# Graph-layer kernel: the left-over sums read all 128 rows of the last chunk, GpSimd zeroes its empty rows, and block A's second layer moves to right behind them

## The chip, the cores and the metric

The kernel runs on one core of one Trainium2 chip. The metric is the device time of the whole kernel in microseconds, over several runs; three runs of the kernel before lie between 277.67 and 277.8 us.

## The reference

There are 12500 nodes with 128 features, 412500 edges with 48 features, and for each edge the number of its receiving node. The edges are sorted by receiver.

```python
h   = jnp.maximum(_layernorm(x), 0.0)
agg = jax.ops.segment_sum(edges, recv, num_segments=12500)    # 48 per node
u   = graph_globals[0]                                         # the same for every node
hid = jax.nn.relu(concat([h, agg, u]) @ W1 + b1)               # 256 per node
out = x + hid @ W2 + b2
```

All numbers are 32-bit floats.

## The kernel before, in words

**Chunks, groups, blocks.** 768 edges are a chunk: it lies in SBUF as 128 rows of 6 edges. Four chunks are a group, loaded by one transfer of 576 KB. Eleven groups and 1024 nodes make an iteration; there are 12 of them (`NIT`), and in each two blocks of 512 nodes, A and B, go through the layers. Behind the 12 iterations come the left-overs: six chunks, five of them whole (`FULL` is 5) and the last with 84 edges, which fill only 14 of its 128 rows (`TP` is 14), and a last block Z of 212 nodes.

**What one iteration does.** VectorE (DVE) writes a one-hot tile per slot of groups (L662: 28 columns, 1 where an edge's receiver has that distance from the chunk's start). TensorE (PE) multiplies it with the edges, six products per chunk, four chunks side by side in four column ranges (L681), so that a PSUM bank S holds sums of the edges by receiver; ScalarE (ACT) copies them out (L685). DVE writes a second kind of one-hot tile, `pl` (L668), which shifts the 28 sums of each chunk to the right place among the iteration's nodes, and PE adds them up in two banks (L703). Beside that the nodes are normalised (DVE, ACT), turned by PE (L740), and go through the first layer (L750 for the nodes, L755 for the sums, `relu` on ACT, L760). The second layer (`second`, L772) is 16 matmul records per block (L776) and an addition on DVE: in the loop it writes the block of the iteration before into `hold` (L780), in the epilogue into `ot` (L778). What it adds is `xb`, the block's input plus the bias b2, which GpSimd (POOL) makes in `add_b` (L735); GpSimd may do so only when the addition of the iteration before has read the old `xb`.

**Stores are kept back.** 11 of the 12 iterations' results stay in SBUF in `hold`, and are stored in the epilogue: `store_held` (L783) issues 22 stores of 256 KB on the SP queue, one behind the other. The last blocks are stored by `store` (L560): A and Z on the SP queue behind those, B on ACT's. So all of the 6.4 MB of output leave in the epilogue.

**What sets the order.** Each operation is recorded by `op(engine, name, reads, writes, ...)`. An engine runs its operations in the order in which they are recorded. A wait is derived from the names: an operation waits for the last writer of what it reads or writes, and for the readers of what it writes. Each engine except PE runs the iterations as a loop and then the epilogue's operations; PE's loop is rotated but comes to the same order. A transfer waits on its issuing engine's queue, and everything behind it on that queue waits with it.

**The epilogue** (L926). `load_rest` (L544) records on SP the transfer `lez`, five whole chunks, 720 KB, into `e[0]`, and then `lezt`, the last chunk's 14 rows, 15.8 KB. `e[0]` is the edge tile of slot 0; `lez` waits until the last iteration's sums over slot 0 (`su0`) have read it. `lezt` names `e0.1` as `lez` does, and so waits until `lez` has landed. Then come the 22 stores. `sur` (L937 to L940) is the left-over sums on PE. Its 36 products, 72 matmul records in the trace, are 24 of the first four chunks and then 6 + 6 of the fifth and the sixth chunk in turn, the latter over 14 rows alone (`rest`, L936). ACT copies them (`ssr`, L941). PE goes on with the last shifted sums of the loop (`place(5, (0,), 0)`), the turning of Z, the shifted left-over sums (`pcr`, L948), Z's first layer, block A's second layer, a transposition for the verdict on whether the sorted edges were dense enough (L632), block B's second layer, and Z's. `verdict_0` and `verdict_1` are small DVE operations.

Of the kernel before, what the change touches and what calls it, by code (L numbers as in the profile page):

```python
# [18 lines left out]
P = 128  # L19
EPS = 1e-5  # L20
T = 6
CE = P * T
CG = 4
# [3 lines left out]
IN = 1024  # L27
# [7 lines left out]
V = 28  # L35
NV = 32
# [16 lines left out]
class Flow:  # L53
# [14 lines left out]
    def op(self, eng, name, reads, writes, emit, dma=False):  # L68
        self.seq.append(dict(eng=eng, name=name, r=tuple(reads), w=tuple(writes), emit=emit, dma=dma, it=self.at))
# [336 lines left out]
def kernel(  # L406
# [12 lines left out]
    nc = tc.nc  # L419
    N, D = x.shape  # L420
    E, DE = edge_attr.shape
# [7 lines left out]
    TP = TAIL // T  # L429
# [14 lines left out]
    def bank(name):  # L444
        return psum.tile([P, BN], F32, name=name)

    S = [bank("s0"), bank("s1")]
    agg = [bank("ax"), bank("ay")]
    pt = bank("pt")
    ph = [bank("ph0"), bank("ph1")]  # L450
# [9 lines left out]
    e = [const.tile([P, len(p) * CG, T * DE], F32, name=f"e{s}") for s, p in enumerate(SLOTS)]  # L460
    oh = [const.tile([P, len(p) * q, V], F32, name=f"oh{s}") for s, p in enumerate(SLOTS)]
# [48 lines left out]
    op = f.op  # L510
    A, B, Z = 0, 1, 2

    def dma(eng, name, reads, writes, dst_ap, src_ap):
        def emit(i):
            with nc.allow_non_contiguous_dma(reason="small pieces"):
                return [f.of[eng].dma_start(dst_ap(i) if callable(dst_ap) else dst_ap, src_ap(i) if callable(src_ap) else src_ap)]  # L516
        op(eng, name, reads, writes, emit, dma=True)
# [24 lines left out]
    FULL = NFULL - (NIT * GI + 1) * CG  # L542

    def load_rest():  # L544
        at = (NIT * GI + 1) * GE
        dma("SP", "lez", [], ["e0.0", "e0.1"], e[0][:, :FULL], edge_attr[at:at + FULL * CE].rearrange("(c p t) d -> p c (t d)", p=P, t=T))
        dma("SP", "lezt", [], ["e0.1", "ezt"], e[0][:TP, FULL], edge_attr[E - TAIL:E].rearrange("(p t) d -> p (t d)", t=T))

    def rows_of(ap, i, a, m, r):
        return span(ap, i, a, m * r).rearrange("(p r) d -> p (r d)", r=r)  # L550
# [9 lines left out]
    def store(k, a, m=P, eng="SP"):  # L560
        r = RR[k]
        dv = ot[k].rearrange("p r d -> p (r d)")
        q = m - m % 16
        dma(eng, f"so{k}", [f"ot{k}"], [], lambda i: rows_of(out, i, a, q, r), dv[:q])
        if q < m:
            dma(eng, f"so{k}t", [f"ot{k}"], [], lambda i: rows_of(out, i, lambda i: a(i) + q * r, m - q, r), dv[q:m])
# [42 lines left out]
    def farthest():  # L609

        op("DVE", "fa", ["rel_i"], ["far"], lambda i: [nc.vector.tensor_reduce(
            far, rel_i.rearrange("p g t -> p (g t)"), AX.X, OP.max, apply_absolute_value=True)])
        op("DVE", "fm", ["far"], ["farm"], lambda i: [nc.vector.tensor_tensor(farm, farm, far, OP.max)])

    def verdict_0():
        v0 = NG - 1
        live = NV * (NCH - v0 * CG)
        vs = [f"vv{b}" for b in range(NB)]
        op("DVE", "w0", vs, ["worst1"], lambda i: [nc.vector.tensor_reduce(worst[:, 0:1], vv[:, :v0], AX.X, OP.max, apply_absolute_value=True)])
        op("DVE", "w1", vs, ["worst2"], lambda i: [nc.vector.tensor_reduce(worst[:live, 1:2], vv[:live, v0:NG], AX.X, OP.max, apply_absolute_value=True)])  # L620
        f.chain("DVE", "w2", ["worst1", "worst2"], ["worst"],
            lambda: nc.vector.tensor_reduce(worst[:, 2:3], worst[:, 0:2], AX.X, OP.max),
            lambda: nc.vector.tensor_scalar(worst[:, 2:3], worst[:, 2:3], -(WIN - V) / 2, None, OP.add))

    def verdict_1():
        farthest()
        f.chain("DVE", "wc", ["worst", "farm"], ["wcol"],
            lambda: nc.vector.tensor_scalar(wcol, farm, -(V - 1) / 2, None, OP.add),
            lambda: nc.vector.tensor_tensor(wcol, wcol, worst[:, 2:3], OP.max))
# [7 lines left out]
    def cols(ap, i, a, n):  # L637
        return ap[:, ds(a(i), n)] if not isinstance(i, int) else ap[:, a(i):a(i) + n]
# [52 lines left out]
    def place(s, fresh=(), part=None):  # L691

        groups, sv, pv = SLOTS[s], ss[s], pl[s]
        todo = [(n, j) + v for j, g in enumerate(groups) for n, v in enumerate(pieces(g)) if part is None or v[0] == part]
        todo.sort(key=lambda v: v[2] if len(groups) == 1 else (v[0] if v[1] == 0 else 1 - v[0], v[1]))
        seen = set()

        def emit(i):
            seen.clear()
            out = []  # L700
            for _, j, bk, at, frm, w in todo:
                h = HI * bk
                out.append(nc.tensor.matmul(agg[bk][h:h + DE, at:at + w], sv[:, j], pv[:, j, frm:frm + w],  # L703
                                            start=bk in fresh and bk not in seen, stop=True, skip_group_check=True))
                seen.add(bk)
            return out
        op("PE", f"pc{s}" + ("" if part is None else f".{part}"), [f"ss{s}", f"pl{s}"], [f"bk{b}" for b in sorted({v[2] for v in todo})], emit)
# [64 lines left out]
    def second(k, m=P, bk=None, key="PO", keep=None):  # L772

        ov = (po if bk is None else bk)[:, :RR[k] * D].rearrange("p (r d) -> p r d", r=RR[k])
        op("PE", f"w2{k}", [f"hid{k}.{a}" for a in range(NH)] + ["w2"], [key], lambda i: [
            nc.tensor.matmul(ov[:m, r], hid[k][:, a, r, :m], w2[:, a], start=(a == 0), stop=(a == NH - 1)) for r in range(RR[k]) for a in range(NH)])  # L776
        if keep is None:
            op("DVE", f"ot{k}", [key, f"xb{k}"], [f"ot{k}"], lambda i: [nc.vector.tensor_tensor(ot[k][:m], ov[:m], xb[k][:m], OP.add)])  # L778
        else:
            op("DVE", f"ho{k}", [key, f"xb{k}"] + (["spare"] if k == A else []), [f"hold{k}.{keep(f.at)}"], lambda i: [nc.vector.tensor_tensor(  # L780
                cols(hold[k], i, lambda i: keep(i) * (R * D), R * D).rearrange("p (r d) -> p r d", r=R), ov, xb[k], OP.add)])
# [144 lines left out]
    def epilogue():  # L926
        f.at = NIT
        m = RN // RZ
        load_rest()
        store_held()  # L930
        add_b(Z, m)
        stats(Z, m)
        variance(Z, m)
        shift(Z, m)
        norm(Z, m)
        rest = lambda j, c: P if j * CG + c < FULL else TP  # L936
        op("PE", "sur", ["oh0", "oh1", "e0.0", "e0.1", "ezt"], ["S0"], lambda i: [  # L937
            nc.tensor.matmul(S[0][NV * c:NV * c + V, j * DE:(j + 1) * DE], oh[j][:rest(j, c), c * T + t], e[0][:rest(j, c), j * CG + c, t * DE:(t + 1) * DE],  # L938
                             start=(t == 0), stop=(t == T - 1), skip_group_check=True)
            for j in range(2) for t in range(T) for c in range(min(CG, RC - j * CG))])  # L940
        op("ACT", "ssr", ["S0"], ["ssr"], lambda i: [nc.scalar.copy(ssr.rearrange("p j d -> p (j d)"), S[0][:, :2 * DE])])  # L941
        place(5, (0,), 0)
        turn(Z, m, S[1], "S1")
        verdict_0()
        verdict_1()
        todo = [(j,) + v for j, g in enumerate((1, 2)) for v in pieces(g)]
        op("PE", "pcr", ["ssr", "pl0", "pl1"], ["bk0"], lambda i: [
            nc.tensor.matmul(agg[bk][:DE, at:at + w], ssr[:, j], pl[j][:, 0, frm:frm + w], start=False, stop=True, skip_group_check=True)  # L948
            for j, bk, at, frm, w in todo])
        sums_out(Z, m)  # L950
        zr = [S[0][:, a * RN:(a + 1) * RN].rearrange("p (r c) -> p r c", r=RZ) for a in range(NH)]
        for a in range(NH):
            layer_x(f"z{a}", "S0", zr[a], Z, a, a == 0, m)
        for a in range(NH):
            layer_e(f"z{a}", "S0", zr[a], Z, a, m)
        for a in range(NH):
            relu(f"z{a}", "S0", zr[a], Z, a, m)
        second(A, P, ph[A], "PH0")
        store(A, lambda i: (i - 1) * IN)
        verdict_2()  # L960
        second(B, P, ph[B], "PH1")
        store(B, lambda i: (i - 1) * IN + BN, eng="ACT")
        second(Z, m, pt, "PT")
        store(Z, lambda i: i * IN, m)
        for e_ in f.of:
            op(e_, f"rb{e_}", ["bad"], [], lambda i, e_=e_: [f.of[e_].reg_load(flag_of[f.of[e_].engine], bad[0:1, 0:1])])
# [48 lines left out]
```

## Time and profile before

| | |
|---|---|
| median of three runs | 277.77 us |
| device time of the profiled execution | 277.39 us |
| its span | 275.6 us |
| granted TensorE clock | 0.973 |
| PE busy | 252.7 us, 92% |
| DVE busy | 239.5 us, 87% |
| ACT busy | 128.2 us, 47% |
| GpSimd busy | 54.5 us, 20% |
| DMA over the span | 94.33 MB, 342 GB/s |

Times in the trace are microseconds from the start of the span. The device time of the same execution is 1.8 us longer than the span. The loop ends at about 258 us for PE, and the epilogue takes the rest. A row of a timeline gives start, duration, engine, line, operation, destination and sources, shape, and how many instructions it stands for. SPq and ACTq rows are the issuing of transfers, not their flight. A row of stretches gives length, busy time of PE, its weight loads, DVE, ACT and GpSimd (instructions in brackets), the granted clock, the mean busy share of the 16 DMA engines, and what they moved in GB/s.

### The profile page before, as it was taken

To read this page: it belongs to the slowest core of one execution; us is meant where nothing else is said; L and a number is where in the kernel's file an instruction comes from. 1 tells how busy PE (TensorE), PEld (TensorE's weight loads), DVE (VectorE), ACT (ScalarE), POOL (GpSimd) and SP (SyncE) were. 2 spreads that over 40 slices of the span, in tenths; PEclk is the share of its full clock that TensorE was granted. 3 is DMA by queue.
4 is the path that set the end of the run, shared out by engine and by line. 5 is a ranking of instruction groups with operands and counts; after the bars stand their busy time and mean duration, and the time that the engine had idled before them with its cause. 6 is when DMAs were issued, how large, how long until landed. Compare 5 with 4: busy or idle time off the path is not lost.

```text
span 275.6 us, 17205 instructions
## 1 busy us (share of the span) xinstructions
PE 252.7 (92%) x7567; PEld 195.6 (71%) x7568; DVE 239.5 (87%) x591; ACT 128.2 (47%) x316; POOL 54.5 (20%) x47
## 2 busy tenths in 40 slices
PE   2946999999999999999999999999999999999990
PEld 2946866867858849859768768578498497597580
DVE  4899997998989989989989979989899899799521
ACT  7800544535437337245445355373373463454520
POOL 8100050040220400500500502304105005007000
PEclk9955999999999999999999999999999999999999
DMA  6999999999999999999999999999999999995992
GB/s 213 297 363 356 341 357 362 356 357 361 356 361 357 356 362 356 356 362 356 356 362 356 356 362 356 359 359 356 362 357 356 362 356 356 362 356 208 368 363 73
DMA packets 79012, 94.33 MB, mean 342 GB/s; under 512 B 3227, under 2 KB 72189, under 8 KB 78998
## 3 DMA queue, kind: packets, MB, share of 16 engines
q1 hardware_dynamic: 75398, 87.63, 96.1%
q10 hardware_dynamic: 3312, 6.03, 6.2%
q0 software_dynamic: 288, 0.49, 0.7%
q8 instruction: 7, 0.11, 0.2%
q14 instruction: 7, 0.06, 0.1%
HBM read 87.75 MB, written 6.40 MB: 342 GB/s over the span
## 4 chain that ended last, share of the span: by engine, by line
PE 87%; SPq 5%; DMA 3%; issue 2%; DVE 0%
PE s L681 27%; PE ph L776 18%; PE ph L750 8%; PE ax L703 7%; SPq L516 5%; PE ph L755 5%; PE po L750 4%; PE pt L750 4%; PE pt L755 4%; DMA e<-in_edge_attr_dram 3%; PE ay L703 3%; PE pt L740 3%; PE po L740 2%; PE s L938 1%; PE s L750 0%
## 5 line engine op out<-in xcount | busy, mean ns | idle before, releaser
L662 DVE TENSOR_TENSOR oh<-iota_v,rel_i 128x1344 f32<-128x1344 f32 (+1 forms) x78 | 130.8, 1716 | 0.0
L681 PEld LDWEIGHTS s<-e,oh 128*28 128x28 f32 x6336 | 75.1, 109 | 23.3 <-issue 21.4
L681 PE MATMUL s<-e,oh 128*28 128x48 f32 x6336 | 80.9, 210 | 11.0 <-issue 6.7
L735 POOL TENSOR_TENSOR xba<-xa,b_sb 128x512 f32<-128x512 f32 x12 | 15.4, 1285 | 198.3 <-DVE holda L780 198.3
L685 ACT COPY ss<-s 128x96 f32<-128x96 f32 (+1 forms) x72 | 16.8, 234 | 70.6 <-PE s L681 70.6
L668 DVE TENSOR_SCALAR pl<-iota_w,off_i 128x186 f32<-128x186 f32 x141 | 35.1, 309 | 0.5
L735 POOL TENSOR_TENSOR xbb<-xb,b_sb 128x512 f32<-128x512 f32 x12 | 31.1, 2591 | 0.0
L760 ACT ACTIVATE hida<-ph,bias 128x512 f32<-128x512 f32 x12 | 8.2, 687 | 42.2 <-PE ph L755 42.2
L703 PE MATMUL ax<-pl,ss 128*48 128x186 f32 (+3 forms) x172 | 27.1, 300 | 0.0
L776 PEld LDWEIGHTS ph<-w,hida 128*128 128x128 f32 x208 | 24.2, 191 | 3.8 <-issue 3.8
L776 PE MATMUL ph<-w,hida 128*128 128x128 f32 x208 | 26.7, 281 | 0.0
L703 PE MATMUL ay<-pl,ss 128*48 128x186 f32 (+3 forms) x168 | 26.3, 297 | 0.0
L776 PE MATMUL ph<-w,hidb 128*128 128x128 f32 x208 | 25.6, 276 | 0.6 <-issue 0.6
L776 PEld LDWEIGHTS ph<-w,hidb 128*128 128x128 f32 x208 | 24.3, 192 | 0.8 <-issue 0.7
L731 ACT ACTIVATE xna<-xa,sha,sca 128x128 f32<-128x128 f32 x48 | 19.8, 482 | 5.1 <-DVE sha L727 5.1
L710 DVE BATCH_NORM_STATS2 sta<-xa 128x6 f32<-128x128 f32 x48 | 10.5, 281 | 12.1 <-DMA xa<-in_x_dram 12.1
L703 PEld LDWEIGHTS ax<-pl,ss 128*48 128x48 f32 x172 | 17.6, 126 | 4.3 <-issue 2.0
L731 ACT ACTIVATE xnb<-xb,shb,scb 128x128 f32<-128x128 f32 x48 | 19.6, 479 | 0.0
L703 PEld LDWEIGHTS ay<-pl,ss 128*48 128x48 f32 x168 | 17.8, 124 | 0.0
L755 PE MATMUL ph<-ags,w1a 48*128 48x512 f32 x48 | 13.5, 641 | 0.0
L750 PE MATMUL ph<-hta,w1h 128*128 128x512 f32 x24 | 13.5, 644 | 0.0
L750 PE MATMUL ph<-htb,w1h 128*128 128x512 f32 x24 | 12.3, 592 | 0.0
(150 smaller groups left out, 301.5 us busy)
## 6 DMA issues: line engine op xcount, KB each, us to landing
e<-in_edge_attr_dram SPq DMA_DIRECT2D x133, 576.0 KB, 10.0
xa<-in_x_dram ACTq DMA_DIRECT2D x11, 256.0 KB, 5.8
xb<-in_x_dram ACTq DMA_DIRECT2D x11, 256.0 KB, 6.3
out_dram<-holda SPq DMA_DIRECT2D x11, 256.0 KB, 3.2
out_dram<-holdb SPq DMA_DIRECT2D x11, 256.0 KB, 3.3
holda<-in_dst_dram SPq DMA_DIRECT2D x4, 384.0 KB, 4.9
e<-in_edge_attr_dram SPq DMA_DIRECT2D x1, 720.0 KB, 8.9
xa<-in_x_dram SPq DMA_DIRECT2D x1, 256.0 KB, 10.5
```

The lines of the kernel that those rows point to most:

```text
L516: return [f.of[eng].dma_start(dst_ap(i) if callable(dst_ap) else dst_ap, src_ap(i) if callable(src_ap) else src_ap)]
L662: op("DVE", f"oh{name}", reads + ["iota_v"], [f"oh{name}"], lambda i: [nc.vector.tensor_tensor(ov, iota_v[:, None, None, :].to_broadcast([ ...
L668: nc.vector.tensor_scalar(out[:, j], iota_w, o[j], None, OP.is_equal) for j in range(len(o))])
L681: nc.tensor.matmul(S[k][NV * c:NV * c + V, j * DE:(j + 1) * DE], o[:, (j * CG + c) * T + t], ev[:, j * CG + c, t * DE:(t + 1) * DE], start ...
L685: op("ACT", f"ss{name}", [f"S{k}"], [f"ss{name}"], lambda i: [nc.scalar.copy(sv.rearrange("p j d -> p (j d)"), S[k][:, :m * DE])])
L703: out.append(nc.tensor.matmul(agg[bk][h:h + DE, at:at + w], sv[:, j], pv[:, j, frm:frm + w], start=bk in fresh and bk not in seen, stop=Tr ...
L731: nc.scalar.activation(xn[k][:m, r], xt[k][:m, r], AF.Relu, bias=sh[k][:m, r:r + 1], scale=sc[k][:m, r:r + 1]) for r in range(RR[k])])
L735: nc.gpsimd.tensor_tensor(xb[k][:m], xt[k][:m], b2_sb[:m, None, :].to_broadcast([m, RR[k], D]), OP.add)])
L740: op("PE", f"tu{k}", [f"xn{k}", "ident"], [key], lambda i: [nc.tensor.transpose(pv[:, r, :m], xn[k][:m, r], ident[:m, :m]) for r in range( ...
L750: nc.tensor.matmul(o, w1h[:, a * P:(a + 1) * P], hT[k][:, :, :m], start=first, stop=False, skip_group_check=True)])
L755: nc.tensor.matmul(o, w1a[h:h + DE, a * P:(a + 1) * P], ag[k // 2][h:h + DE, :, :m], start=False, stop=True, skip_group_check=True)])
L776: nc.tensor.matmul(ov[:m, r], hid[k][:, a, r, :m], w2[:, a], start=(a == 0), stop=(a == NH - 1)) for r in range(RR[k]) for a in range(NH)])
```

## The change

A GpSimd operation `ezz` is recorded first in the epilogue. It fills the sixth chunk's place in `e[0]`, 128 rows of 288 numbers, with zeros. It writes the name `e0.1`, so that `lez`, which writes the same name, comes behind it. `sur` then multiplies all 128 rows of each chunk. The two first verdict operations, block A's second layer and its store stand right behind `sur` and its copy, ahead of the last shifted sums and the turning of Z.

```diff
     def epilogue():
         f.at = NIT
         m = RN // RZ
+        op("POOL", "ezz", [], ["e0.1"], lambda i: [nc.gpsimd.memset(e[0][:, FULL], 0.0)])
         load_rest()
         store_held()
...
-        rest = lambda j, c: P if j * CG + c < FULL else TP
         op("PE", "sur", ["oh0", "oh1", "e0.0", "e0.1", "ezt"], ["S0"], lambda i: [
-            nc.tensor.matmul(S[0][NV * c:NV * c + V, j * DE:(j + 1) * DE], oh[j][:rest(j, c), c * T + t], e[0][:rest(j, c), j * CG + c, t * DE:(t + 1) * DE],
+            nc.tensor.matmul(S[0][NV * c:NV * c + V, j * DE:(j + 1) * DE], oh[j][:, c * T + t], e[0][:, j * CG + c, t * DE:(t + 1) * DE],
                              start=(t == 0), stop=(t == T - 1), skip_group_check=True)
             for j in range(2) for t in range(T) for c in range(min(CG, RC - j * CG))])
         op("ACT", "ssr", ["S0"], ["ssr"], lambda i: [nc.scalar.copy(ssr.rearrange("p j d -> p (j d)"), S[0][:, :2 * DE])])
+        verdict_0()
+        verdict_1()
+        second(A, P, ph[A], "PH0")
+        store(A, lambda i: (i - 1) * IN)
         place(5, (0,), 0)
         turn(Z, m, S[1], "S1")
-        verdict_0()
-        verdict_1()
...
-        second(A, P, ph[A], "PH0")
-        store(A, lambda i: (i - 1) * IN)
         verdict_2()
```

GpSimd's program from the last part of its loop into the epilogue, before. `xba` and `xbb` are the two additions of the loop, which wait for `ho0` and `ho1`, DVE's additions of the second layer; `xbr` is that of block Z.

```order
L735 TENSOR_TENSOR xba<-xa,b_sb 128x512 [waits ho0]
L735 TENSOR_TENSOR xbb<-xb,b_sb 128x512 [waits ho1]
L224 REGISTER_ALU
L746 UNCONDITIONAL_BRANCH
L230 REGISTER_ALU
L230 COMPARE_AND_BRANCH
L735 TENSOR_TENSOR xbr<-xr,b_sb 106x256 [waits lx2,lx2t]
```

The same place in the changed kernel:

```order
L735 TENSOR_TENSOR xba<-xa,b_sb 128x512 [waits ho0]
L735 TENSOR_TENSOR xbb<-xb,b_sb 128x512 [waits ho1]
L224 REGISTER_ALU
L746 UNCONDITIONAL_BRANCH
L230 REGISTER_ALU
L230 COMPARE_AND_BRANCH
L929 MEMSET e_80 128x288
L735 TENSOR_TENSOR xbr<-xr,b_sb 106x256 [waits lx2,lx2t]
```

The zeroing, L929, stands behind both additions of the last iteration.

SP's program at the start of the epilogue, before. `e_80` is `e[0]`; the first transfer is `lez`, the second `lezt`, and the stores of `hold` follow.

```order
L230 COMPARE_AND_BRANCH
L516 DMA e_80<-in_edge_attr_dram 128x5x288 [waits su0]
L516 DMA e_80<-in_edge_attr_dram 14x288 [waits lez]
L516 DMA out_dram<-holda 128x512
L516 DMA out_dram<-holdb 128x512
```

The same place in the changed kernel:

```order
L230 COMPARE_AND_BRANCH
L516 DMA e_80<-in_edge_attr_dram 128x5x288 [waits POOL]
L516 DMA e_80<-in_edge_attr_dram 14x288 [waits lez]
L516 DMA out_dram<-holda 128x512
L516 DMA out_dram<-holdb 128x512
```

`lez` waits for GpSimd's zeroing where it waited for PE's sums over slot 0; the order of the queue is the same.

PE's program in the epilogue, as a difference: `hida` is block A's hidden layer, `ph_70` the bank of its second layer.

```order
 L938 MATMUL s_65<-e_80,oh_86 28x48 x23
 L938 MATMUL s_65<-e_80,oh_87 28x48 x12
+L776 MATMUL ph_70<-w_142,hida 128x128 [waits hi0_1]
+L776 MATMUL ph_70<-w_142,hida 128x128 x7
 L703 MATMUL ax<-pl_97,ss_103 48x140
...
 L755 MATMUL s_65<-agr,w1a 128x212 [waits ACT]
 L755 MATMUL s_65<-agr,w1a 128x212
-L776 MATMUL ph_70<-w_142,hida 128x128 x8
 L632 MATMUL s_66<-ident,wcol 1x128 [waits DVE]
 L776 MATMUL ph_71<-w_142,hidb 128x128 x8
```

Block A's second layer has moved from behind Z's first layer to right behind the left-over sums. DVE's and ACT's programs have the same order as before.

## The prediction

> **What bounds the kernel now.** I read the page first, then the last 25 us. Here are the page's row of GB/s in 40 slices, its totals, and the head of the chain of work that ended last.
>
> ```profile
> GB/s 213 297 363 356 341 357 362 356 357 361 356 361 357 356 362 356 356 362 356 356 362 356 356 362 356 359 359 356 362 357 356 362 356 356 362 356 208 368 363 73
> HBM read 87.75 MB, written 6.40 MB: 342 GB/s over the span
> PE 87%; SPq 5%; DMA 3%; issue 2%; DVE 0%
> ```
>
> The chain is PE's nearly all the way, but that is a share of the whole span. The GB/s row shows two stages: loads until slice 36, a dip, and then 368 and 363 again. Behind the dip it is the output that moves: all 6.40 MB of it leave in the last 24 us. So the last stage has two candidates for its end, PE and the transfers. The rows of stretches of that stage, busy time per engine, then DMA share and GB/s:
>
> ```profile
> 246.00:247.00 1.00, 1.00 (x11) 1.00 (x11) 0.93 (x5) 0.16 (x1) 0.00 (x0) 1.00 1.09 355
> 251.20:252.00 0.80, 0.80 (x11) 0.58 (x10) 0.80 (x2) 0.75 (x2) 0.80 (x1) 1.00 0.00 0
> 252.00:252.40 0.40, 0.40 (x10) 0.34 (x7) 0.40 (x1) 0.32 (x1) 0.40 (x2) 1.00 0.18 40
> 252.40:267.80 15.40, 15.40 (x144) 10.03 (x139) 7.48 (x26) 6.19 (x14) 1.27 (x1) 1.00 0.99 374
> 267.80:268.20 0.40, 0.40 (x6) 0.40 (x6) 0.00 (x0) 0.00 (x0) 0.00 (x0) 1.00 0.26 97
> 268.20:269.00 0.80, 0.80 (x10) 0.80 (x9) 0.40 (x1) 0.00 (x0) 0.00 (x0) 1.00 0.88 333
> 269.00:270.00 1.00, 0.44 (x5) 0.23 (x3) 0.72 (x2) 0.00 (x0) 0.00 (x0) 1.00 0.01 4
> 270.20:271.40 1.20, 0.00 (x0) 0.00 (x0) 0.00 (x0) 0.00 (x0) 0.00 (x0) 1.00 0.91 306
> ```
>
> From 252.4 to 267.8 the DMA engines are full (share 0.99, 374 GB/s: 5.76 MB, which are the 22 kept stores). Only then do they idle: 0.3 us up to 268.2, 1.0 us up to 270.0. That is the whole reserve of the transfers. Now the issuing rows of the same stage, from the timeline:
>
> ```profile
> 242.25 0.72 SPq L516 DMA_DIRECT2D e<-in_edge_attr_dram  x1
> 251.22 0.36 SPq L516 DMA_DIRECT2D e<-in_edge_attr_dram  x1
> 251.62 0.37 SPq L516 DMA_DIRECT2D out_dram<-holda  x1
> 265.67 0.64 SPq L516 DMA_DIRECT2D out_dram<-holdb  x1
> 267.43 0.33 SPq L516 DMA_DIRECT2D out_dram<-ota  x1
> 269.48 0.43 DVE L778 TENSOR_TENSOR otr<-pt,xbr 106x256 f32<-106x256 f32 x1 [0.18 <-PE pt L776]
> 269.93 0.77 SPq L516 DMA_DIRECT2D out_dram<-otr  x2
> L976 SPq EVENT_SEMAPHORE  x1: 28/28/28, 272.0 to 272.0; - x1
> ```
>
> The load `lez` is issued at 242.25, in the loop's shadow; `lezt` waits for its landing until 251.22; the first kept store follows at 251.62, the last at 265.67; then SP waits for PE and DVE: A's result goes at 267.43, Z's at 269.93, and SP sees everything landed at 272.0. From there to the end of the span, 275.6, nothing is left but closing semaphores. So PE sets the end before, but the stores are only some 1.6 us behind it. SP's waits say the same:
>
> ```profile
> SPq L516 <- DMA e<-in_edge_attr_dram: 8.2, 1, 8.2
> SPq L516 <- DVE otr L778: 2.2, 1, 2.2
> ```
>
> SP's 8.2 us for `lez` cost nothing as long as the load is issued at 242; the DMA engines are still busy with edges (share 1.09 at 246).
>
> **The change part by part.** The zeroing comes first on GpSimd's epilogue. GpSimd and DVE in the last iteration:
>
> ```profile
> 248.53 1.28 POOL L735 TENSOR_TENSOR xba<-xa,b_sb 128x512 f32<-128x512 f32 x1 [15.69 <-DVE holda L780]
> 249.77 2.59 POOL L735 TENSOR_TENSOR xbb<-xb,b_sb 128x512 f32<-128x512 f32 x1
> 252.33 1.34 POOL L735 TENSOR_TENSOR xbr<-xr,b_sb 106x256 f32<-106x256 f32 x1
> 248.96 6.12 DVE L662 TENSOR_TENSOR oh<-iota_v,rel_i 128x1344 f32<-128x1344 f32 x3
> ```
>
> GpSimd stands idle for 15.69 us before `xba`, which waits for DVE's `holda`, but its program is in order: the zeroing comes behind `xbb`, at 249.77 + 2.59 = 252.36, where `xbr` starts today. `lez` waits for it, 10 us later than now. What a zeroing takes on GpSimd, from the groups by line:
>
> ```profile
> L802 POOL MEMSET ident<- 128x128 f32 x1 | 0.2, 204 | 0.5 <-SPq L980 0.5
> L820 POOL MEMSET rel<- 128x228 f32 x1 | 0.3, 307 | 0.0
> ```
>
> 100 columns more cost 103 ns, so 288 columns take about 0.37 us: it ends at 252.73. SP issues 0.02 us behind what it waits for (`otr` ends at 269.48 + 0.43 = 269.91, the store goes at 269.93), so `lez` goes at about 252.76. `xbr` shifts by 0.37 us; it is needed only for `otr` at 269.48, so that is hidden.
>
> How long `lez` flies on idle DMA engines no row shows directly. The nearest landings, and the first transfer of the program with the first DVE instruction that waited for it:
>
> ```profile
> e<-in_edge_attr_dram SPq DMA_DIRECT2D x1, 720.0 KB, 8.9
> out_dram<-ota SPq DMA_DIRECT2D x1, 256.0 KB, 2.2
> out_dram<-otr SPq DMA_DIRECT2D x1, 96.0 KB, 1.9
> 1.01 3.61 SPq L516 DMA_DIRECT2D holda<-in_dst_dram  x7
> 4.15 0.15 DVE L579 CAST fc<-holda 128x1 f32<-128x1 int32 x1 [1.21 <-DMA holda<-in_dst_dram]
> ```
>
> The 8.9 us of `lez` itself include a queue of edges in front of it, which has drained by 251.2 (share 0.00), so they are out as its price here. From below: 2.2 us for 256 KB, plus 464 KB more at 374 GB/s, 1.3 us, is 3.5. From above: the first 384 KB came in 4.15 - 1.01 = 3.1 us; 344 KB more at 355 GB/s, the rate of edge loads, are 1.0 us, so 4.1. By parts: the first store's bytes move at 252.4, 0.8 us after its issue; 737280 bytes at 355 GB/s take 2.1; and 0.6 us pass between the last bytes (271.4) and SP's seeing them (272.0): 3.5. I take **3.6 us**, near the two that agree and come from the same stage. `lez` has landed at 256.4, `lezt` is issued, and 0.4 us behind it (251.22 to 251.62) the first kept store: at 256.8 in place of 251.62, **5.2 us late**.
>
> The Trainium skill (DMA: Bandwidth & Descriptors, section Latency and other measured facts) puts the first byte of a transfer issued from SP at about 0.6 us, where this trace shows 0.8; by its figure, an estimate, load and first store would each be 0.2 us earlier and the total 0.4 us less. The rows decide here.
>
> What of the 5.2 us is absorbed? The transfers' idle time before the end: 0.3 us to 268.2, 0.1 to 269.0, 1.0 to 270.0 and 0.2 to 270.2, together 1.6. So the end comes 5.2 - 1.6 = 3.6 us later. The other way: 6.40 MB at 374 GB/s are 17.1 us; from 256.8 + 0.8 they end at 274.7, and SP sees it at 275.3, 3.3 us behind 272.0. I take **3.4 us**.
>
> Now PE. How the left-over sums run, as stretches of L938 alone, and beside them 144 records of full rows in the loop:
>
> ```profile
> 258.30:258.80 0.50, 0.42 (x39) 0.42 (x43) 1.00 0.99 365
> 259.80:260.30 0.50, 0.50 (x7) 0.29 (x7) 1.00 0.62 225
> 258.38 2.94 PE L938 MATMUL s<-e,oh 128*28 128x48 f32 x72
> 248.89 1.73 PE L681 MATMUL s<-e,oh 128*28 128x48 f32 x144 [0.41 <-issue]
> ```
>
> The first 48 records run as in the loop, 39 in 0.42 us; the 24 in which full and 14-row products take turns run at about 7 per half microsecond and take most of the 2.94 us. With full rows throughout they cost at best 24 x 12 ns = 0.3 us, so PE gains between nothing and 1.6 us; I take 1.5. Block A's second layer in front of the turn adds no work, and fills time in which PE waits for ACT. **None of this reaches the end**: the stores cover it. SP now comes to Z's store 265.67 + 0.64 - 251.62 = 14.7 us after its first store, plus one more for A: at 256.8 + 14.7 + 0.3 = 271.8, while `otr` has been ready since 269.91 or earlier. If that cover were gone, PE's gain would be worth about 2 us. `sur` waits for `lezt`, issued at 256.4; with the 1.9 us in which 96 KB land it is there at 258.3, just as PE comes to it (258.38). A stall of some tenths there eats into PE's gain only.
>
> Sum: span 275.6 + 3.4 = 279.0; with the 1.8 us around the span, 277.39 + 3.4 = **280.8 us**. The profiled execution is 0.38 us below the median of 277.77, so against that it is 1.1% slower.
>
> **The rivals.**
>
> *The load isn't late (faster).* If GpSimd came to its zeroing in its 15.69 us of idle time, the first store would go at 251.6 as now and PE would decide. PE would be done 1.5 us earlier by `sur` and some 0.5 us by waits filled, and the stores would then end without a gap, 1.6 to 1.9 us earlier than now (the two sums above less the 5.2 us). That is 277.39 - 1.7 = 275.7 us. It decides if the first store is issued before 251.62 + 1.7 = 253.3; for that GpSimd would have to reach the zeroing by 248.9. The order of its program and the row of `xbb` speak against it: 3 in 100. Within half a microsecond of 253.3 no change would be seen: 2 in 100.
>
> *DVE holds the zeroing up (slower still).* `xbb` took 2.59 us for the work that took `xba` 1.28, while DVE ran its long one-hot operations. If the zeroing too were stopped until these end at 248.96 + 6.12 = 255.08, it would end 2.4 us later than I reckon: 283.2 us. The Trainium skill (SBUF — State Buffer, section Who interferes with whom) says that a DVE instruction with two SBUF inputs holds up GpSimd instructions that read SBUF, not those that only write. The trace agrees in `xbb`, which reads; the zeroing only writes, so by that rule it goes through. No row here shows a zeroing beside such an operation: 6 in 100.
>
> *PE decides even so.* If `lezt` landed 2 us later than 258.3, `sur` and all behind it would shift, and `otr` would come after 271.8: 281 to 283 us. 2 in 100.
>
> **How the numbers follow.** Forecast 87 in 100, the rivals 3, 2, 6 and 2. The range: `lez` flying 3.5 to 4.1 us, a zeroing between 0.2 and 0.8, 3.3 or 3.6 us for the stores, 0.4 us between this execution and the median: 279.7 to 282.2, with a little room to the next rival, 279.6 to 282.4. A difference under 0.2% can't be told from none here. Faster 0.03, same 0.02, slower 0.95.
>
> **What would show it right or wrong.** In the changed profile: the zeroing at 252.4; `lez` issued at 252.8 and a dip to nothing in GB/s from 251 to 253.5, a hump of loads, and a second dip near 256 to 257.5; the first kept store at 256.8; GB/s full until the end, with SP never waiting for `otr`; the chain ending in transfers in place of PE; L938 in about 1.3 us. It is wrong if `lez` is issued before 250, or if SP still waits for DVE's `otr` at the end.

## The result, and the profile after

The changed kernel takes 282.53 us (282.4 to 282.56, four runs); the kernel before took 277.72 in the same series. The ratio is 1.0175, with a 95% interval of 1.0157 to 1.0193: slower by 4.8 us. I had said slower, 280.8 us, with a range up to 282.4; the time lies 0.13 us above it. The profiled execution took 282.51 us, its span is 280.7.

First rows of the changed kernel's timeline around the end of the loop and at the end, of GpSimd, of DVE and of SP's queue; the last row is SP's wait for the last landing:

```profile
249.10 6.11 DVE L662 TENSOR_TENSOR oh<-iota_v,rel_i 128x1344 f32<-128x1344 f32 x3
249.91 2.59 POOL L735 TENSOR_TENSOR xbb<-xb,b_sb 128x512 f32<-128x512 f32 x1
252.44 0.33 POOL L929 MEMSET e<- 128x288 f32 x1
252.81 0.38 SPq L516 DMA_DIRECT2D e<-in_edge_attr_dram  x1
257.30 0.36 SPq L516 DMA_DIRECT2D e<-in_edge_attr_dram  x1
257.70 0.37 SPq L516 DMA_DIRECT2D out_dram<-holda  x1
268.35 0.42 DVE L778 TENSOR_TENSOR otr<-pt,xbr 106x256 f32<-106x256 f32 x1 [0.18 <-PE pt L776]
272.11 0.63 SPq L516 DMA_DIRECT2D out_dram<-holdb  x1
273.48 1.65 SPq L516 DMA_DIRECT2D out_dram<-otr  x2
L976 SPq EVENT_SEMAPHORE  x1: 28/28/28, 277.0 to 277.0; - x1
```

The zeroing runs from 252.44 to 252.77, `lez` goes at 252.81 in place of 242.25, `lezt` at 257.30, and the first kept store at 257.70 in place of 251.62. Block Z's result lies ready at 268.35 + 0.42 = 268.77, earlier than before, and waits until 273.48 for its turn on the queue. SP sees the last landing at 277.0 in place of 272.0.

What SP waited for says it in three rows:

```profile
SPq L516 <- POOL e L929: 10.7, 1, 10.7
SPq L516 <- DMA e<-in_edge_attr_dram: 4.1, 1, 4.1
SPq L976 <- DMA out_dram<-otr: 0.4, 1, 0.4
```

The wait for DVE's `otr` is gone. A wait of 10.7 us for the zeroing has come ahead of everything, and the wait for the load, 8.2 us before, is shorter and now lies in the open. The page's row of GB/s shows the hole:

```profile
GB/s 214 293 365 358 344 357 361 356 359 359 356 362 356 356 362 356 356 362 356 358 360 356 361 357 356 362 356 356 362 356 357 361 356 361 357 90 164 377 383 107
PE 75%; DMA 8%; SPq 5%; DVE 4%; issue 3%; POOL 1%; ACT 0%; POOLq 0%; DVEq 0%; ACTq 0%
```

Slices 36 and 37, 246 to 260 us, are at 90 and 164 where 357 to 360 would be full. The chain in the second row is still mostly PE's: its last links in order of time are PE's product for Z at 267.44 us and DVE's addition behind it, done at 268.77, some eight microseconds before the last landing. It doesn't follow the stores that stand in SP's queue. Whoever reads only that chain would look for the loss on PE. In the stretches one sees the hole and its edges:

```profile
248.00:249.00 1.00, 0.55 (x55) 0.45 (x42) 1.00 (x2) 0.24 (x1) 0.33 (x1) 1.00 0.11 37
249.00:250.00 1.00, 1.00 (x97) 1.00 (x101) 1.00 (x2) 0.20 (x1) 1.00 (x2) 1.00 0.00 0
253.60:254.00 0.40, 0.40 (x3) 0.16 (x2) 0.40 (x1) 0.29 (x1) 0.20 (x1) 1.00 0.20 32
254.00:254.40 0.40, 0.40 (x3) 0.16 (x2) 0.40 (x1) 0.00 (x0) 0.00 (x0) 1.00 0.82 150
254.40:254.80 0.40, 0.40 (x3) 0.16 (x2) 0.40 (x1) 0.00 (x0) 0.00 (x0) 1.00 0.60 84
255.20:255.60 0.40, 0.40 (x3) 0.16 (x2) 0.40 (x4) 0.00 (x0) 0.00 (x0) 1.00 1.08 389
256.80:257.20 0.40, 0.40 (x4) 0.16 (x4) 0.37 (x3) 0.00 (x0) 0.00 (x0) 1.00 0.00 0
258.80:275.20 16.40, 9.43 (x131) 7.98 (x131) 3.83 (x15) 3.94 (x11) 0.00 (x0) 0.90 1.02 379
275.20:275.60 0.40, 0.00 (x0) 0.00 (x0) 0.00 (x0) 0.00 (x0) 0.00 (x0) 0.50 0.75 223
275.60:276.00 0.40, 0.00 (x0) 0.00 (x0) 0.00 (x0) 0.00 (x0) 0.00 (x0) 0.50 0.24 79
258.40:276.40 18.00, 9.55 (x133) 7.98 (x131) 3.83 (x15) 4.34 (x11) 0.00 (x0) 0.87 0.96 357
```

The edges' last bytes are through by 249; the load's first come at about 253.9 and trickle at 32 to 150 GB/s for a microsecond before the rate is full; then comes a second hole, 256.8 to 258, while `lezt` waits for the load's landing and the first store for its issue; then the output runs at 379 GB/s and dies away from 275.2 to 276.4. The last row is the whole stretch of the output: 18.0 us at 357 GB/s on the mean.

### The profile page after: what moved, and what is told of

Its sections match the earlier page's. It is cut to its first block, busy times and chain, and to the rows that moved or that the text cites. A ratio compares the mean times of both kernels' runs of the same rounds, so it can differ in the third digit from the quotient of the medians.

```text
span 280.7 us, 17204 instructions
## 1 busy us (share of the span) xinstructions
PE 251.5 (90%) x7567; PEld 194.7 (69%) x7568; DVE 239.5 (85%) x591; ACT 128.3 (46%) x316; POOL 54.5 (19%) x48
## 4 chain that ended last, share of the span: by engine, by line
PE 75%; DMA 8%; SPq 5%; DVE 4%; issue 3%; POOL 1%; ACT 0%; POOLq 0%; DVEq 0%; ACTq 0%
PE s L681 24%; PE ph L776 16%; PE ph L750 7%; PE ax L703 6%; DMA e<-in_edge_attr_dram 6%; SPq L516 5%; PE ph L755 4%; PE pt L750 3%; PE po L750 3%; PE pt L755 3%; PE ay L703 3%; PE pt L740 2%; DMA xa<-in_x_dram 2%; DVE oh L662 2%; PE po L740 2%
## 5 line engine op out<-in xcount | busy, mean ns | idle before, releaser
L681 PEld LDWEIGHTS s<-e,oh 128*28 128x28 f32 x6336 | 75.1, 109 | 21.4 <-issue 19.5
L776 PEld LDWEIGHTS ph<-w,hidb 128*128 128x128 f32 x208 | 24.3, 192 | 0.4 <-issue 0.4
L731 ACT ACTIVATE xnb<-xb,shb,scb 128x128 f32<-128x128 f32 x48 | 19.6, 478 | 0.0
```

The lines of the kernel that those rows point to most:

```text
L681: nc.tensor.matmul(S[k][NV * c:NV * c + V, j * DE:(j + 1) * DE], o[:, (j * CG + c) * T + t], ev[:, j * CG + c, t * DE:(t + 1) * DE], start ...
L731: nc.scalar.activation(xn[k][:m, r], xt[k][:m, r], AF.Relu, bias=sh[k][:m, r:r + 1], scale=sc[k][:m, r:r + 1]) for r in range(RR[k])])
```

## The experiments

Two theories stood at the start. **S**: the kept stores, behind the late load on SP's queue, set the end. **W**: the changed work itself does, by the moved layer, the sums or their later start on PE. Times of different executions drift by up to 1.5 us in the loop (`xbb` ends between 252.04 and 253.53), and the kernel before has medians from 277.72 to 278.47 in the different series; so beside the median and the ratio to the kernel before in the same series I give **tail**: from the end of GpSimd's last addition in the loop (`xbb`: start and duration) to SP's seeing the last landing. For the kernel before it is 272.0 - 252.36 = 19.6 us, for the change 277.0 - 252.50 = 24.5.

| kernel | median us | ratio (95% interval) | tail us |
|---|---|---|---|
| zeroing alone | 283.44 | 1.0174 (1.0126 to 1.0221) | 24.4 |
| full rows alone | 278.05 | 0.9999 (0.9966 to 1.0032) | 19.5 |
| order alone | 278.07 | 0.9987 (0.9968 to 1.0005) | 19.6 |
| change without zeroing | 276.75 | 0.9932 (0.99 to 0.9963) | 18.3 |
| own tile, zeroed early | 276.25 | 0.9942 (0.9929 to 0.9956) | 17.9 |
| own tile, zeroing kept late | 281.04 | 1.0113 (1.0098 to 1.0129) | 22.2 |
| one chunk loaded | 280.33 | 1.0085 (1.0066 to 1.0104) | 22.1 |
| small transfer ahead | 283.05 | 1.0181 (1.0166 to 1.0196) | 24.8 |
| load on GpSimd's queue | 286.19 | 1.0286 (1.0251 to 1.0321) | 28.9 |
| stores first | 288.22 | 1.0372 (1.0335 to 1.0408) | 29.1 |
| long pieces | 282.6 | 1.0156 (1.0126 to 1.0187) | 24.3 |
| six stores first | 279.05 | 1.0018 (0.9998 to 1.0038) | 20.5 |

### The parts one by one

The zeroing alone, in the kernel before:

```diff
         m = RN // RZ
+        op("POOL", "ezz", [], ["e0.1"], lambda i: [nc.gpsimd.memset(e[0][:, FULL], 0.0)])
         load_rest()
```

> The kernel before with the zeroing on GpSimd alone; sums over 14 rows and block A's second layer stay where they were. Theory S (the kept stores, which stand behind the left-over load on SP's queue, set the end): the whole loss is here, 282.3 to 282.9 us, first kept store at about 257.7, SP sees the last landing near 277. Theory W (the moved second layer or the sums that start later on TensorE set the end): near 277.7 us.

It gives the whole loss: 1.0174 against 1.0175, tail 24.4 against 24.5. The median of 283.44 us lies above the expected range, but the kernel before took 278.3 in this series. Its left-over sums, Z's result and Z's store:

```profile
259.96 2.94 PE L939 MATMUL s<-e,oh 128*28 128x48 f32 x72 [0.64 <-DMA e<-in_edge_attr_dram]
271.06 0.43 DVE L778 TENSOR_TENSOR otr<-pt,xbr 106x256 f32<-106x256 f32 x1 [0.18 <-PE pt L776]
274.50 1.69 SPq L516 DMA_DIRECT2D out_dram<-otr  x2
```

The sums still take 2.94 us, and Z's result is ready at 271.49, later than in the change, yet it still waits 3.0 us for its turn on the queue. So neither the moved layer nor the full rows have any part in the loss. The third part of W, the later start of the sums, is in this kernel too, but a result that waits 3.0 us for the queue doesn't set the end. So W is out.

Full rows alone, without a zeroing:

```diff
-nc.tensor.matmul(..., oh[j][:rest(j, c), c * T + t], e[0][:rest(j, c), j * CG + c, ...
+nc.tensor.matmul(..., oh[j][:, c * T + t], e[0][:, j * CG + c, ...
```

> The kernel before with full rows in the left-over sums and no zeroing: rows 14 to 127 of the last chunk hold edges of the loop and are added too. S: no wait is added, TensorE still sets the end and saves what the 24 mixed records cost, so 276.2 to 276.8 us, left-over sums in 1.2 us instead of 2.9. W: 277.7 us or more.

The sums fell as expected, the time did not: 278.05 us, ratio 0.9999. Timeline of PE and ACT behind the sums:

```profile
259.04 1.21 PE L937 MATMUL s<-e,oh 128*28 128x48 f32 x72
260.18 0.53 PE L703 MATMUL ax<-pl,ss 128*48 128x140 f32 x4
261.32 0.88 ACT L731 ACTIVATE xnr<-xr,shr,scr 106x128 f32<-106x128 f32 x2 [0.43 <-DVE shr L727]
262.25 0.40 PE L740 MATMUL s<-ident,xnr 106*128 106x106 f32 x2 [1.54 <-ACT xnr L731]
```

The 1.7 us saved turn into a wait of 1.54 us: PE, early at the turning of Z, stands until ACT has normalised Z at 262.2. My expectation of 276.2 to 276.8 us had overlooked that wait.

The order alone:

```diff
+        verdict_0()
+        verdict_1()
+        second(A, P, ph[A], "PH0")
+        store(A, lambda i: (i - 1) * IN)
         place(5, (0,), 0)
...
-        second(A, P, ph[A], "PH0")
-        store(A, lambda i: (i - 1) * IN)
         verdict_2()
```

> The kernel before with the two verdict operations and block A's second layer moved alone. S: it fills waits of TensorE for ScalarE, 277.0 to 277.7 us. W: the move itself costs, 279 us or more.

278.07 us, ratio 0.9987 with 1 inside the interval: nothing that can be told from no change, where I had expected up to 1 us less. The turning of Z in the kernel before shows why:

```profile
261.70 0.40 PE L740 MATMUL s<-ident,xnr 106*128 106x106 f32 x2
```

It has no wait in front of it, since the slow sums, and the shifted sums behind them, last until ACT has normalised Z. The moved layer finds nothing to fill.

Both together, without the zeroing:

```diff
-        op("POOL", "ezz", [], ["e0.1"], lambda i: [nc.gpsimd.memset(e[0][:, FULL], 0.0)])
         load_rest()
```

> The changed kernel without the zeroing: full rows and the moved second layer; rows 14 to 127 of the last chunk hold edges of the loop and are added too. S: the load goes early again, TensorE is done about 2 us earlier and the stores' own end decides, 275.7 to 276.3 us. W: 281 us or more, as with the zeroing.

276.75 us, ratio 0.9932: faster by some 1.9 us, tail 1.3 us shorter. The time lies above the 275.7 to 276.3 expected; the gain is near the 2 us that I had named for PE. Two edits that give nothing each give this together, because block A's second layer stands exactly in the wait that the faster sums run into: the same four places of PE and ACT as above, in this kernel:

```profile
258.57 1.21 PE L937 MATMUL s<-e,oh 128*28 128x48 f32 x72
259.71 2.05 PE L776 MATMUL ph<-w,hida 128*128 128x128 f32 x16
260.84 0.88 ACT L731 ACTIVATE xnr<-xr,shr,scr 106x128 f32<-106x128 f32 x2 [0.43 <-DVE shr L727]
262.15 0.40 PE L740 MATMUL s<-ident,xnr 106*128 106x106 f32 x2
```

The turning of Z now comes without a wait.

### The gain without the wait

The last chunk gets a tile of its own, zeroed in GpSimd's prologue; its 14 rows then wait neither for the zeroing nor for `lez`.

```diff
+    ez = const.tile([P, T * DE], F32)
...
-        dma("SP", "lezt", [], ["e0.1", "ezt"], e[0][:TP, FULL], edge_attr[E - TAIL:E]...
+        dma("SP", "lezt", [], ["ezt"], ez[:TP], edge_attr[E - TAIL:E]...
...
+        pool("ezp", ["ezt"], lambda: nc.gpsimd.memset(ez, 0.0))
...
-        op("POOL", "ezz", [], ["e0.1"], lambda i: [nc.gpsimd.memset(e[0][:, FULL], 0.0)])
...
-e[0][:, j * CG + c, t * DE:(t + 1) * DE]
+(e[0][:, j * CG + c] if j * CG + c < FULL else ez)[:, t * DE:(t + 1) * DE]
```

> The changed kernel with the last chunk in a tile of its own that GpSimd zeroes in the prologue. The load of the five chunks waits for TensorE's sums again, and the 14 rows no longer wait for that load, so the kept stores are issued near 243. S: TensorE alone sets the end, with the gain of the full rows and of the moved layer: 0.5 to 0.9% faster than before, 275.3 to 276.4 us; the stores are through by 266. W: 281 us or more.

276.25 us, ratio 0.9942: faster than both kernels, by 1.6 us than the one before. Its first kept store goes at 245.22 (near 243 expected), and at the end SP waits for DVE alone:

```profile
SPq L517 <- DVE otr L779: 5.1, 1, 5.1
SPq L517 <- DVE ota L779: 1.1, 1, 1.1
```

PE sets the end, and the stores have over 5 us of room. Now the same kernel with the zeroing put back into the epilogue, where only `lez` waits for it:

```diff
         m = RN // RZ
+        op("POOL", "ezz", [], ["e0.1"], lambda i: [nc.gpsimd.memset(e[0][:, FULL], 0.0)])
         load_rest()
```

> The same tile of its own, but the zeroing stays in the epilogue too, where nothing needs it except that the load of the five chunks waits for it as in the changed kernel. The first kept store is issued right behind that load, at about 253.3, in place of 257.7. S: the end comes 4.4 us earlier than in the changed kernel, 277.8 to 278.6 us, about what it was before. W (late sums on TensorE set the end): they still wait for the load until about 257.5, so 282 us.

281.04 us. Its first kept store, and a stretch that lies in the change's second hole:

```profile
254.02 0.37 SPq L517 DMA_DIRECT2D out_dram<-holda  x1
257.00:258.00 1.00, 1.00 (x6) 0.48 (x6) 0.56 (x4) 0.04 (x1) 0.00 (x0) 1.00 1.07 405
```

The first kept store came at 254.02, 3.7 us earlier than in the change, but the end only by 1.5 us in the median and 2.3 in the tail. The time is neither the 278 us of S nor the 282 of W. So S as I had put it fails: the end does not follow the first store one for one. Stores issued right behind the load share the DMA engines with it, and the load's 720 KB still have to pass. What is saved is the second hole: here the engines move 405 GB/s where the change moves nothing. By the shares of the change's stretches from 256.4 to 258.8, the engines lose about 2.0 us there, an estimate; the tail gains 2.3. The currency is not a place in a queue but the time in which the DMA engines stand idle or half idle while 7.1 MB still have to go.

### The late load, put elsewhere

Both loads on GpSimd's queue, the kept stores free on SP's:

```diff
-        dma("SP", "lez", ...
+        dma("POOL", "lez", ...
-        dma("SP", "lezt", ...
+        dma("POOL", "lezt", ...
```

> The changed kernel with both left-over loads issued from GpSimd's own queue, right behind its zeroing; SP issues the kept stores as soon as its loop is done, near 243. The load is as late as in the changed kernel, only the stores no longer stand behind it. S: the load shares the DMA engines with the stores, lands at 258 to 260, TensorE is late by at most 1 us and sets the end: 276 to 278.5 us. Theory L (a late load costs the same whoever waits behind it): 281 us or more.

286.19 us: far from S's number, and beyond L's 281. The stores are issued from 242 on and fill the engines, and the loads have to push through them: the rows of transfers say 8.5 us for the 720 KB and 4.6 for the 15.8 KB.

```profile
e<-in_edge_attr_dram POOLq DMA_DIRECT2D x1, 720.0 KB, 8.5
e<-in_edge_attr_dram POOLq DMA_DIRECT2D x1, 15.8 KB, 4.6
266.04 2.13 PE L938 MATMUL s<-e,oh 128*28 128x48 f32 x72 [7.95 <-DMA e<-in_edge_attr_dram]
268.10 3.79 PE L776 MATMUL ph<-w,hida 128*128 128x128 f32 x16
```

PE waits 7.95 us for the left-over edges, and is slow when they come (more on that below). The other order on SP's queue:

```diff
-        load_rest()
         store_held()
+        load_rest()
```

> The changed kernel with the 22 kept stores ahead of the two left-over loads on SP's queue. Now the load stands behind 5.77 MB of stores. S, read the other way round: the stores are through at about 264, the load lands at 266.4 and its 14 rows at 268.2, the left-over sums start 9.4 us later than in the changed kernel, and TensorE's work behind them sets the end: 284 to 287 us, slower than the changed kernel. If only the stores' place in the queue counted, 276 us.

288.22 us, tail 29.1: slower than the change, as expected, but above the 284 to 287 that I had named. The sums start at 267.53. So a late load has two prices, and one can only choose which to pay: ahead of the stores it delays them, behind them it delays PE.

Between the two lies a third way, six stores ahead of the load, which fit into the idle time:

```diff
+        store_held(range(3))
         load_rest()
-        store_held()
+        store_held(range(3, NIT - 1))
```

> The changed kernel with six of the 22 kept stores ahead of the left-over loads on SP's queue, and 16 behind. The zeroing and the load stay as late as they are. Theory I (what the late zeroing costs is the time in which the DMA engines stand idle, 248.4 to 253.9): six stores, 1.57 MB, fill 4.1 us of it, the load is not crowded out because they are through when it is issued, and the end comes 4.1 us earlier than in the changed kernel: 278.0 to 278.9 us. Theory L (a late load costs the same whatever else moves): 281 us or more.

The median is 279.05, 0.15 us above the expected range; against the kernel before on the same chip it is 1.0018, with 1 inside the interval, where the change has 1.0175. The tail is 4.0 us shorter than the change's, 4.1 expected. Stretches of this kernel, its load, and SP's wait for Z's result:

```profile
249.00:250.00 1.00, 0.60 (x56) 0.49 (x46) 1.00 (x3) 0.24 (x1) 0.58 (x1) 1.00 1.06 400
250.00:251.00 1.00, 1.00 (x113) 1.00 (x104) 1.00 (x1) 0.20 (x1) 1.00 (x2) 1.00 0.96 356
253.56 4.96 SPq L516 DMA_DIRECT2D e<-in_edge_attr_dram  x2
e<-in_edge_attr_dram SPq DMA_DIRECT2D x1, 720.0 KB, 4.6
SPq L516 <- DVE otr L778: 0.6, 1, 0.6
```

The hole at 249 is filled, the zeroing and the load are as late as in the change (issue at 253.56, flight 4.6 us), and nearly the whole loss against the kernel before is gone. That shows theory I: the loss is the DMA engines' idle time, not the lateness of the load. The last row says what comes next: SP waits 0.6 us for Z's result, so PE and the transfers now end nearly together. The tail stays 2.2 us longer than without the zeroing (18.3): the sums start 0.7 us later after `xbb`'s end (6.5 us for 5.7), and the second hole ahead of the kept stores is still there. What each of the two costs isn't shown.

### How long the load flies

The price of `lez` was the uncertain term of the sum. One chunk in place of five:

```diff
-e[0][:, :FULL], edge_attr[at:at + FULL * CE]...
+e[0][:, :1], edge_attr[at:at + CE]...
```

> The changed kernel, but the load brings one chunk, 144 KB, in place of five, 720 KB; the other four chunks' sums are of old data. If the 4.5 us of the load are a long start and then the full rate (2.6 us and 390 GB/s), this one lands after 3.0 us and the kernel takes 281.0 us; if they are a short start (1.4 us) and a low rate of 238 GB/s throughout, it lands after 2.0 us: 280.0 us. W: no change, 282.5.

The kernel took 280.33 us, between the two expected times, and the load landed after 2.2 us, the last number of its row:

```profile
e<-in_edge_attr_dram SPq DMA_DIRECT2D x1, 144.0 KB, 2.2
```

The 576 KB less save 2.3 us, 256 GB/s on the mean, and the fixed part is about 1.6 us: near the second of the two forms. But neither is the whole truth, since the change's stretches above show a slow first microsecond and then the full rate. The 144 KB fit into that microsecond: in this kernel's stretches the load moves from 253.6 to 254.8, at no more than 190 GB/s. Does that first microsecond come from the queues' having been idle? The test is a small transfer right ahead:

```diff
-        dma("SP", "lez", [], ["e0.0", "e0.1"], ...
-        dma("SP", "lezt", [], ["e0.1", "ezt"], ...
+        dma("SP", "lew", [], ["e0.1"], e[0][:TP, FULL + 1], edge_attr[E - TAIL:E]...
+        dma("SP", "lez", [], ["e0.0"], ...
+        dma("SP", "lezt", [], ["e0.0", "ezt"], ...
```

`lew` now waits for the zeroing, `lez` stands right behind it on the queue without a wait for it, and `lezt` still waits for `lez`.

> The changed kernel with one more transfer of 15.8 KB right ahead of the load, also behind the zeroing, into a place that nothing reads. If the load starts slowly because the queues had been idle for 4 us, the small one takes the start on itself and the load lands 3.6 us after its own issue: 282.0 us in all. If the slow start is the load's own, it lands 4.5 us after its issue: 282.9 us.

The load's row in this kernel:

```profile
e<-in_edge_attr_dram SPq DMA_DIRECT2D x1, 720.0 KB, 4.5
```

4.5 us from its own issue, as in the change, and 283.05 us: the small one, 0.4 us ahead, takes nothing off it. Does the slow start come from the 640 short pieces?

```diff
-e[0][:, :FULL], edge_attr[...].rearrange("(c p t) d -> p c (t d)", p=P, t=T)
+e[0][:, :FULL].rearrange("p c d -> p (c d)"), edge_attr[...].rearrange("(p t) d -> p (t d)", t=FULL * T)
```

> The changed kernel, but the load reads its 720 KB as 128 pieces of 5760 bytes in place of 640 pieces of 1152 bytes, so that edges come to other rows than their one-hot rows and the left-over sums are of wrongly placed edges. If the slow first microsecond of the load comes from the many short pieces, the load lands after 3.5 us and the kernel takes 281.5 us; if it is the start of any read on idle engines, it lands after 4.4 us: 282.5 us.

The row once more:

```profile
e<-in_edge_attr_dram SPq DMA_DIRECT2D x1, 720.0 KB, 4.4
```

4.4 us, and 282.6 us for the kernel: no. Pieces five times as long are as slow to start. So a read of 720 KB that found the engines idle, or nearly so, took 4.4 to 4.6 us in the five kernels in which no store was issued right behind it. Why the first microsecond is slow is not settled; a small transfer that goes more than 0.4 us ahead of the load wasn't tried.

## Why the prediction was right in kind and too small in size

- **The zeroing** was to end at 252.73 and `lez` to go at 252.76; they did so at 252.77 and 252.81. Right, and so was the rule that let it through beside DVE's one-hot operations, which ran from 249.10 to 255.21: 0.33 us, not the 2.7 of that rival. The Trainium skill (SBUF — State Buffer, section Who interferes with whom) has it that only GpSimd instructions that read are held up by a DVE instruction with two SBUF inputs; the zeroing, which only writes, agrees.
- **The flight of `lez`** is the first step that failed: 3.6 us forecast, 4.5 measured, above even the 4.1 at the end of the range. Of the three sums I took the two that rested on stores, and set aside the one that rested on a load, 4.1 us from the program's first transfer (its 344 KB should be 336, which leaves the 1.0 us as it is). In parts, the load took 1.0 us to its first bytes for 0.8, 3.0 us for its data (to 256.8) for 2.1, and 0.5 us to its landing for 0.6. A load on idle engines has a slow first microsecond (32, 150, 84 GB/s above) that the stores hardly have. The 0.8 us were misread for the store, too: in stretches of 0.1 us its first bytes move 0.5 us after its issue, in both kernels, and only the fuller rate comes at about 0.8.
- **The 17.1 us for the output** are the second step that failed, a term too small: from 258.4 to 276.4 they are 18.0 us. The steady rate was as taken, 379 for 374 GB/s; what I left out is above all the end, where the engines finish unevenly, 0.75 and then 0.24 of them busy, as they do at the end of the loads in the kernel before (its share falls from 1.03 at 248.4 to 0 at 250.8). By the other way: 6.1 us late, of which 1.1 were absorbed, not 1.6.
- Together 0.9 + 0.9 us, less 0.1 by which the first store's bytes came earlier: 1.7 us more at SP's last landing, 5.0 for 3.3. That is all of the miss.
- **PE's gain and the cover.** The sums took 1.21 us, as said (about 1.3); that is 1.73 us less than before, a little over the 1.6 that I had given as the most. `lezt` was in a little later than said, so that they began at 258.89 for 258.3. Nothing of it reached the end: right, and the kernel without the zeroing and the one with its own tile show the gain to be 1.9 and 1.6 us where the cover is gone (about 2 us were named).
- **The rivals.** That the load isn't late, and PE decides, was worth 275.7 us; the kernel without the zeroing came to 276.75 and the one with its own tile to 276.25. DVE's lock and a PE that decides did not happen.
- **What would show it** held in kind: the dip, the hump, the second dip, and SP never waiting for `otr`. The dip began at 249 in place of 251, and the first kept store went at 257.70 in place of 256.8. One point did not hold: the chain did not end in transfers. That view does not follow a queue; SP's waits do.

Reading the mechanism as "the first store is late" was too narrow, though it gave the sign. Only the kernel with its own tile and the late zeroing, and the one with six stores first, told it from "the DMA engines are idle".

## What to carry to other kernels

A write to a buffer that a load will fill is a wait in front of that load; look where the writing engine stands in its own program, not at how idle it is. The instruction took 0.33 us and cost 4.8, because it stood behind two additions that end 10 us after the load's old place. Against the same change without it (276.75 us, tail 18.3 for 24.5) it cost about 6, since it also hid the gain on PE. Where a transfer moves out of a full queue into an empty one, price its flight by a transfer of the same direction that started on idle engines, and count the uneven end of a long queue. A tile of its own, prepared early, kept the queues apart here and brought the gain of 1.6 us.

## What was not expected of the hardware

The granted clock. In the kernel with the loads on GpSimd's queue PE is idle from 258.1 to 266.0. Stretches of it; the granted clock is the third number from the end:

```profile
260.00:262.00 2.00, 0.00 (x0) 0.00 (x0) 1.79 (x10) 0.88 (x2) 0.60 (x2) 1.00 1.05 406
262.00:264.00 2.00, 0.00 (x0) 0.00 (x0) 0.69 (x1) 0.00 (x0) 0.66 (x1) 0.51 0.94 359
270.00:272.00 2.00, 2.00 (x10) 1.78 (x10) 0.08 (x1) 0.00 (x0) 0.00 (x0) 0.50 0.00 0
272.00:274.00 2.00, 2.00 (x12) 1.42 (x12) 0.61 (x1) 0.66 (x2) 0.00 (x0) 0.93 0.26 99
```

It falls to 0.50 some 4 us after PE's last matmul and comes back only about 6 us after the work does: block A's second layer runs from 268.1 and takes 3.79 us there, 2.05 in the kernel before. The sums take 2.13 us there, 1.21 in the change. So a wait of 8 us on PE cost some 2.7 us more behind it, in these two groups alone. Neither time is the same in every run. In the kernel with all stores first, PE stands still from 258.4 to 267.5; the clock falls 2.9 us after the last matmul, and is back 3.9 us after the work. At the end of the program, in the fourteen profiles, it falls between 2.3 and 5.2 us after the last matmul. The Trainium skill (TensorE: Matmul & The Clock Gate, Part 1) gives an idle window of about 3.4 us, and the falls lie on both sides of that; for the way back it gives about as long, and here it took 6.2 and 3.9.
